# Two bursts of 38 and 40 down products in place of three (22, 32, 24) in the FP4 feed-forward stage

## The chip, the cores and the metric

The kernel runs on one core of a Trainium2 chip. That core has a tensor engine (PE in the profile, its weight loads PEld), a vector engine (DVE), a scalar engine (ACT), a general engine (POOL), each with its own instruction queue, and DMA queues (SP issues most transfers). The metric is the device time of one execution in microseconds.

## The reference, cut to what matters

The model has two layers on x of 2 x 1024 rows of 512. The change lies in the first layer's feed-forward block, whose weights are stored as 4-bit codes with one scale per group of 128 inputs:

```python
w_gu   = dequant_fp4(gate_up_packed, gate_up_scales)   # [2*1408, 512]
w_down = dequant_fp4(down_packed, down_scales)         # [512, 1408]
gate, up = split(x @ w_gu.T)                           # 1408 columns each
h = silu(gate) * up
y = h @ w_down.T
x = layernorm(x + y / sqrt(mean(y*y) + 1e-6))
```

Before it stands a linear attention, after it a second layer (gated linear attention, then a feed-forward over the top 512 rows of each sequence). Neither is touched.

## The kernel before, in words

**Blocks and steps.** The 2048 rows are four blocks of 512 (`blk`, NB = 4). In each block the 1408 hidden columns are eleven steps of 128 (`f`, NI = 11). A step (`scaled_sums`, L727) makes one 128x512 tile of gate and one of up. Each is a sum over four groups `k` of 128 inputs, and each group has its own scale, so each group's product goes to a PSUM bank of its own: two matmuls (the row tile is split into a high and a low part) and then an eviction. A step is thus 8 banks and 16 matmuls in the order gate, up for k = 0, 1, 2, 3. The evictions of k = 0 are on ACT (L740), those of k = 1 to 3 on DVE (L746: scale and add to the tile), six a step. Where `by_three` holds, the last one of up goes instead by ACT (L743) into a spare tile and by POOL (L744) into the sum. It holds in block 0 for the odd steps and from step 8 on, in blocks 1 and 2 from step 8 on, and never in block 3.

**Banks and rooms.** In this stage the ring `mm` has six of the eight PSUM banks and `acc` two (L903). A bank can be written again when its eviction is done, so the PE can be at most six banks ahead. Gate and up tiles have two rooms in blocks 1 to 3, taken in turn (L914): step f writes where step f-2 wrote, and so waits for the product that read it.

**End of a step.** ACT takes the SiLU of gate (L935), POOL multiplies it with up into `h` (L936, written `hm` below, `hm(3)` for step 3).

**Down products.** The down product of a block is done by a seven-product scheme (`down`, L771) while the next block's steps run. It is a generator that gives one matmul at a time, 78 in all: P1 10, P2 12, P5 10, P4 12, P6 10, P7 10, P3 12, P8 2. Its operands are sums of blocks of h that POOL makes, five instructions a sum (L797): S before P1, and after P5 (the first of them overwrites what P5 reads) three more sums, 15 instructions. It also needs sums of the down weights (`T1`, `T2`, `T4` and a new B12, eight POOL instructions, `sums_of_wdn` L722), made in steps 0 to 3 of block 1. Each P has one `acc` bank, in turn, so P5 uses P1's and P4 uses P2's. ACT copies P1 to y (L803), DVE adds the others (L805 to L827). The y tile of all blocks is one place.

**What sets the order.** The program writes it out: `issue_after` puts each step's matmuls behind the one before on PE, and the work below behind the step's last matmul, eviction, SiLU and `hm`. Apart from such edges each engine's order follows the order of the program among what is ready, as a scheduler fixes it before the run. At f = 0 one call starts `down` (the sums S). Then come the bursts:

```python
if blk > 1 and f in old_steps:
    old_steps[f]()
if blk and f in (1, 4, 7):
    take(pieces, {1: 22, 4: 32, 7: 24}[f])
    mm = last_p[0]
```

In blocks 2 and 3 `old_steps` (L883) finishes the block two before: at f = 0 the squares of y on ACT (L860) and their power on POOL (L864, L865); at f = 1 scaled y on ACT (L869) and four adds to x on POOL (`to_x`, L874); at f = 4 the row statistics on DVE (L187, L188); at f = 7 the normalisation of four tiles on POOL (L839 on DVE, L840, L843). At f = 8 and 9 the next block's rows are turned and split (L196, L210, L211), or in block 3 turned for the next stage (L652). After block 3 its own down products follow in seven parts of another order (L1000), which the change leaves as it is.

## Time and profile before

| | us |
|---|---|
| median of 3 runs (lowest to highest) | 966.21 (965.07 to 968.18) |
| the profiled execution, its own time | 965.93 |
| its span in the profile | 963.8 |
| step 2 to 4 of block 2, gate and up products | 371.47 to 382.86 |
| its second burst, 32 matmuls asked for | 382.86 to 396.49 |
| steps 5 to 7 | 396.49 to 407.88 |
| its third burst, 24 matmuls asked for | 407.88 to 418.05 |
| steps 8 to 10, and 0 and 1 of block 3 | 418.05 to 438.39 |

Each float32 matmul of the down products shows as two matmul records in the trace (22 asked for are 44 records). The PE's records overlap, as matmuls are pipelined: how long one occupies the engine is read from the distance of the starts, not from its duration. In a line of the timeline stand the start, the time from the first start to the last end, the engine, the source line, what is written from what, the count, and in brackets how long the engine had been idle and what released it.

### The profile page before, as it was taken

How to read it: one execution, taken by the hardware profiler on the slowest of the kernel's cores; microseconds unless marked ns; L12 is line 12 of the kernel's file. 1: busy time of each engine (PE TensorE's matmuls, PEld its weight loads, DVE VectorE, ACT ScalarE, POOL GpSimd, SP SyncE). 2: the span in 40 equal slices, each digit the busy share in tenths (PEclk: the TensorE clock that was granted, in tenths of full speed). 3: DMA queues.
4: the chain of work that ended last, by engine and by line, in shares of the span. 5: the costliest groups of instructions: out<-in, count | busy, mean ns of one | idle time of the engine just before them, and what ended most of it. 6: DMA issues, size and time to landing. Idle time of an engine off the chain costs nothing. (4 is left out here: it accounts for less than half of the span.)

```text
span 963.8 us, 11530 instructions
## 1 busy us (share of the span) xinstructions
PE 948.5 (98%) x4261; PEld 753.1 (78%) x4261; DVE 706.4 (73%) x1343; ACT 290.8 (30%) x498; POOL 310.5 (32%) x278
## 2 busy tenths in 40 slices
PE   9999999999999999999999999999999999999996
PEld 6668876785788888888887866778758688888886
DVE  3569986887995676676669485584997795898635
ACT  2244333342552254245133323322122033220000
POOL 1110184003787445576557320101052021000022
PEclk9999999999999999999999999999999999999999
DMA  9622212200000000000011230000005302150011
GB/s 325 211 76 89 83 57 68 67 1 0 2 1 1 1 1 1 1 1 1 1 44 45 100 141 1 1 1 0 1 29 168 110 22 67 45 175 1 1 44 44
DMA packets 25978, 48.77 MB, mean 51 GB/s; under 512 B 4684, under 2 KB 6732, under 8 KB 25411
## 3 DMA queue, kind: packets, MB, share of 16 engines
q1 hardware_dynamic: 23283, 42.92, 13.2%
q0 software_dynamic: 1920, 4.22, 1.2%
q10 hardware_dynamic: 720, 0.92, 0.3%
q8 instruction: 33, 0.54, 0.2%
q14 instruction: 22, 0.18, 0.1%
HBM read 39.63 MB, written 10.52 MB: 52 GB/s over the span
## 5 line engine op out<-in xcount | busy, mean ns | idle before, releaser
L180 POOL TENSOR_TENSOR rs<-rs,table 128x4 f32<-128x4 f32 (+1 forms) x21 | 19.7, 937 | 296.8 <-DVE rs L179 296.5
L746 DVE SCALAR_TENSOR_TENSOR gate<-gatep,scale,gate 128x512 f32<-128x512 f32 x123 | 91.4, 743 | 6.3 <-PE gatep L735 5.9
L746 DVE SCALAR_TENSOR_TENSOR up<-upp,scale,up 128x512 f32<-128x512 f32 x112 | 83.1, 742 | 0.1
L735 PE MATMUL gatep<-x1Th,wgu 128*128 128x512 f32 x176 | 72.4, 411 | 0.6 <-DVE x1Tl L211 0.6
L735 PE MATMUL upp<-x1Th,wgu 128*128 128x512 f32 x176 | 70.4, 400 | 0.1
L735 PE MATMUL upp<-x1Tl,wgu 128*128 128x512 f32 x176 | 69.0, 392 | 0.0
L735 PE MATMUL gatep<-x1Tl,wgu 128*128 128x512 f32 x176 | 68.9, 392 | 0.0
L740 ACT ACTIVATE gate<-gatep,scale 128x512 f32<-128x512 f32 x41 | 28.3, 691 | 110.3 <-PE gatep L735 104.0
L936 POOL TENSOR_TENSOR h<-up,gate 128x512 f32<-128x512 f32 x30 | 39.2, 1308 | 68.3 <-ACT gate L935 63.0
L782 PE MATMUL P<-wdn,h 128*128 128x256 f32 x256 | 60.5, 379 | 0.0
L782 PEld LDWEIGHTS P<-wdn,h 128*128 128x128 f32 x256 | 48.4, 190 | 6.7
L1150 POOL TENSOR_TENSOR sum<-sum,sq 128x512 f32<-128x512 f32 x12 | 19.7, 1644 | 80.4 <-issue 66.3
L1180 PE MATMUL go<-big 128*128 128x256 f32 x192 | 43.7, 381 | 0.0
L366 PE MATMUL xk<-pair,x 128*128 128x512 f32 x96 | 42.7, 592 | 0.0
L187 DVE BATCH_NORM_STATS2 st<-x 128x6 f32<-128x512 f32 x64 | 42.0, 674 | 0.4
L735 PEld LDWEIGHTS upp<-x1Th,wgu 128*128 128x128 f32 x176 | 33.0, 188 | 11.6 <-DVE up L746 3.6
L1180 PEld LDWEIGHTS go<-big 128*128 128x128 f32 x192 | 35.9, 190 | 5.8 <-issue 1.2
L735 PEld LDWEIGHTS gatep<-x1Th,wgu 128*128 128x128 f32 x176 | 33.1, 188 | 9.2 <-DVE gate L746 2.1
L735 PEld LDWEIGHTS upp<-x1Tl,wgu 128*128 128x128 f32 x176 | 33.1, 188 | 6.4 <-issue 0.2
L735 PEld LDWEIGHTS gatep<-x1Tl,wgu 128*128 128x128 f32 x176 | 33.1, 188 | 6.0
L782 PE MATMUL P<-T,S 128*128 128x256 f32 x160 | 35.8, 379 | 0.0
L782 PEld LDWEIGHTS P<-T,S 128*128 128x128 f32 x160 | 30.3, 190 | 4.2
(489 smaller groups left out, 2266.4 us busy)
## 6 DMA issues: line engine op xcount, KB each, us to landing
pk<-in_gu SPq DMA_DIRECT2D x16, 352.0 KB, 3.7
x<-in_x SPq DMA_DIRECT2D x4, 1024.0 KB, 13.0
w<-in_w SPq DMA_DIRECT2D x1, 4096.0 KB, 14.6
xs<-picked SPq DMA_DIRECT2D x4, 1024.0 KB, 5.1
out<-x SPq DMA_DIRECT2D x4, 1024.0 KB, 4.3
w<-in_w SPq DMA_DIRECT2D x4, 1024.0 KB, 7.3
x0T<-in_xT SPq DMA_DIRECT2D x3, 1024.0 KB, 7.9
pk<-in_dn SPq DMA_DIRECT2D x11, 256.0 KB, 3.4
```

The lines of the kernel that those rows point to most:

```text
L180: power = nc.gpsimd.tensor_tensor(rs[:, :n], rs[:, :n], const("mhalf")[:, :n], ALU.pow).ins
L187: nc.vector.bn_stats(st, x)
L366: ins = nc.tensor.matmul(acc_of[b][c], x_t[blk][:, i, c * P : (c + 1) * P], pairs_of["k", blk][i // 2][:, i % 2], start=blk % 2 == 0 and i ...
L735: ins = nc.tensor.matmul(ps, wgu[:, k, at * P : (at + 1) * P], x[:, k], start=x is parts[0], stop=x is parts[1]).ins
L740: nc.scalar.activation(acc, ps, AF.Copy, scale=s)
L746: last = nc.vector.scalar_tensor_tensor(acc, ps, s, acc, ALU.mult, ALU.add).ins
L782: last_p[0] = nc.tensor.matmul(cut, x(j)[:, r], w[:, j], start=j == 0, stop=j == NP - 1 and tail is None).ins
L936: hm = nc.gpsimd.tensor_mul(h.chunk(f), up, gate).ins
L1150: nc.gpsimd.tensor_add(sum2, sum2, sq)
L1180: ins = nc.tensor.matmul(ps[:, 256 * m : 256 * m + 256], w[:, k, m], b[:, k, 256 * half : 256 * half + 256], start=first and m == 0 and k ...
```

## The change

The three bursts behind steps 1, 4 and 7 become two behind steps 2 and 6, of 38 and 40 matmuls. The 78 matmuls are the same and in the same order. The first burst is now P1, P2, P5 and the first half of P4; the second is the rest of P4, then P6, P7, P3 and P8. What `take` draws from the generator besides matmuls moves with them: the evictions, and POOL's 15 sums behind P5, which now come at step 2 and not at step 4. The `old_steps` stay at 0, 1, 4 and 7.

```diff
-                    if blk and f in (1, 4, 7):
-                        take(pieces, {1: 22, 4: 32, 7: 24}[f])
+                    if blk and f in (2, 6):
+                        take(pieces, {2: 38, 6: 40}[f])
                         mm = last_p[0]
```

## The prediction

> **What bounds the kernel now.** First the page's busy shares and its costliest groups:

> ```profile
> PE 948.5 (98%) x4261; PEld 753.1 (78%) x4261; DVE 706.4 (73%) x1343; ACT 290.8 (30%) x498; POOL 310.5 (32%) x278
> ...
> L746 DVE SCALAR_TENSOR_TENSOR gate<-gatep,scale,gate 128x512 f32<-128x512 f32 x123 | 91.4, 743 | 6.3 <-PE gatep L735 5.9
> L746 DVE SCALAR_TENSOR_TENSOR up<-upp,scale,up 128x512 f32<-128x512 f32 x112 | 83.1, 742 | 0.1
> ```

> PE is never free, so nothing can be won by filling it; and the evictions on DVE wait for PE almost nowhere. Whether PE is at its own pace must be read by stretch. The busy time by stretch, for steps 2 to 4 of block 2 and the burst after them (columns: stretch, its length, then busy time of PE, PEld, DVE, ACT, POOL):

> ```profile
> 371.47:382.86 11.39, 11.39 (x50) 9.02 (x49) 10.23 (x16) 5.43 (x9) 2.61 (x2) 1.00 0.00 1
> 382.86:396.49 13.63, 13.63 (x66) 12.00 (x64) 6.34 (x14) 0.63 (x1) 11.10 (x17) 1.00 0.00 1
> ```

> In steps DVE is nearly as full as PE; in the burst it works 6.3 of 13.6 us. The timeline inside the steps shows who leads (start, length):

> ```profile
> 380.57 0.75 DVE L746 SCALAR_TENSOR_TENSOR up<-upp,scale,up 128x512 f32<-128x512 f32 x1
> ...
> 381.37 0.19 PEld L735 LDWEIGHTS upp<-x1Th,wgu 128*128 128x128 f32 x1 [0.36 <-DVE up L746]
> 381.37 0.50 PE L735 MATMUL upp<-x1Th,wgu 128*128 128x512 f32 x1
> ```

> The weight load waits for an eviction that began 0.80 us earlier and ends at 381.32: PE has run six banks ahead and is out of banks.

> **Paces.** Undisturbed gate and up matmuls start 0.2267 us apart in the timeline, so a bank takes PE 0.453 and a step of eight 3.63. DVE's evictions start 0.66 apart: six are 3.96. **In a step PE gains 0.33 us on DVE, and a burst is where DVE catches up.** After a burst the first DVE eviction starts 1.85 after the run's start (371.47, 373.32), an eviction ends 0.75 after its start, and PE writes bank n as soon as bank n-6 is out (0.05 later in the lines above). Changing from a burst to steps costs 0.19 (first two starts 371.47 and 371.89, 0.42 for 0.23). A run of three steps takes 11.39 for 3 x 3.63 + 0.19 = 11.08: 0.3 lost. A down matmul is 0.43 (32 in 13.63).

> **Part by part.** Removed: one switch per block, 3 x 0.19 = -0.6, and the two three-step runs' losses, 6 x 0.3 = -1.8. Work on no engine is removed or added. What moves:

> *Run between the bursts, steps 3 to 6.* Four steps: DVE's eviction number j (from 0) ends at 2.6 + 0.66 j. The last one that PE still needs is that of bank 24 (j = 17), 13.8; bank 30 follows, and three banks later the run ends: 13.87 + 1.36 = 15.2, against 4 x 3.63 + 0.19 = 14.7. **Block 1: +0.5.** In blocks 2 and 3 the row statistics of step 4 come on top. Before, they lie under the burst:

> ```profile
> 384.52 0.75 DVE L746 SCALAR_TENSOR_TENSOR up<-upp,scale,up 128x512 f32<-128x512 f32 x1
> 385.17 1.28 DVE L187 BATCH_NORM_STATS2 st<-x 128x6 f32<-128x512 f32 x2
> ...
> 387.77 0.65 DVE L807 TENSOR_TENSOR y<-y,P 128x512 f32<-128x512 f32 x1
> ```

> From 385.17 to 387.77, and a last aggregate of 0.1: 2.7 us. Queued behind them on DVE are the evictions of steps 5 and 6, for which PE waits. Bank 24 is then out at 16.5 and the run ends at 17.9, 3.2 over 14.7. The order on DVE matters little: the work is the same 4 x 3.96 + 2.7 before the run can end. **Blocks 2 and 3: 2 x 3.2 = +6.4.**

> *Normalisation of step 7, blocks 2 and 3.* Before, it starts in the third burst, and POOL's next work comes only 2.3 us after it:

> ```profile
> 410.42 1.28 POOL L936 TENSOR_TENSOR h<-up,gate 128x512 f32<-128x512 f32 x1 [2.52 <-DVE rs L839]
> 411.66 1.02 POOL L840 TENSOR_TENSOR rs<-rs,table 128x4 f32<-128x4 f32 x1
> 412.79 8.26 POOL L843 TENSOR_SCALAR x<-x,mv,rs 128x512 f32<-128x512 f32 x4
> 423.36 1.30 POOL L744 TENSOR_TENSOR up<-up,b 128x512 f32<-128x512 f32 x1 [2.32 <-ACT b L743]
> 425.57 1.30 POOL L936 TENSOR_TENSOR h_even<-up,gate 128x512 f32<-128x512 f32 x1 [0.91 <-ACT gate L935]
> ```

> Now steps 8, 9 and 10 follow at once. Count from the second burst's end. hm(7) starts at 6.4 (the hm of a first step after a burst: 371.47 to 377.85) and ends at 7.65, the power at 8.7; the four tiles fill 8.8 to 17.05. Behind them stand in block 2 the sum of L744 (1.25) and hm(8) (1.3): hm(8) ends at 19.6. Step 10 writes into the room that hm(8) reads, so ACT's k = 0 eviction of gate waits until then and ends 0.7 later, 20.35. PE reaches step 10 at 3.82 + 4.49 + 4.59 = 12.9 (steps 8 and 9 with their transposes: 418.05, 422.73, 427.32, less the switch), and its seventh bank, which needs the first one's room, 6 x 0.453 later, at 15.6. It waits until 20.4: **+4.8**. In block 3 there is no sum of L744: 19.15 for 15.6, **+3.5**.

> *Run over the block's edge, steps 7 to 2.* It grows by one step at each end. DVE waits 0.23 for PE at 432.73, at step 0, so lag from before it is gone there; steps 0, 1 and 2 are then a three-step run, +0.3 in blocks 1 and 2. In block 3 it starts full after the stall, +0.7. In blocks 2 and 3 the squares of step 0 keep ACT until 1.7 after step 1's end, over the k = 0 evictions of step 2 (due 0.7 after it): nothing if the SiLU of step 1 lets them first, 0.4 if not; I take the half, 2 x 0.2. **+1.7 in all.**

> *POOL's 15 sums* come two steps earlier. In the trace they run from 386.66 to 396.96, 10.3 us. The first may start once P5's second half has read its operand: 22 + 6 matmuls into the burst, 12.1, so they end at 22.4, 6.0 after the burst's end of 38 x 0.4314 = 16.4. The next on POOL, hm(3), is ready 6.4 after it. Free; without that cover they would hold hm(3) and, from two steps on, PE. In block 1 the five weight sums of step 1 end at 297.76, P5 starts only at 285.96 + 3.83 + 9.5 = 299.3: free.

> *The y tile.* P1's copy must wait for `to_x`:

> ```profile
> 371.49 0.59 ACT L803 COPY y<-P 128x512 f32<-128x512 f32 x1 [3.62 <-POOL x L874]
> ...
> 372.10 0.69 DVE L805 TENSOR_TENSOR y<-y,P 128x512 f32<-128x512 f32 x1 [7.61 <-ACT y L803]
> ```

> These 7.6 us of DVE look like the thing to win. They lie under the burst (ended 371.47), and DVE's next eviction still waited 0.53 for PE: the gain is 0. What is new is that P5 reuses P1's bank in the same burst. It starts at 365.8 + 9.5 = 375.3, the copy ends some 372.1: free, with 3 us to spare.

> **Sum.** -0.6 - 1.8 + 0.5 + 6.4 + 4.8 + 3.5 + 1.7 = +14.5. On the profiled execution's own 965.93 (its span and 2.1 around it) that is 980.4; it stood 0.3 under the median shown, so I predict 980.5. The matmuls after block 3 follow the steps without a gap, so I let all of it reach the end. Uncertain are the two POOL stalls (0 to 10 together: the order on POOL) and the half I took for the squares.

> **Rivals.**

> *POOL's order slips.* The order is fixed before the run by what is ready then. For it: on ACT the k = 0 evictions of a step stand ahead of the SiLU before. Against: all four tiles are ready together when the power is done, and stand earlier in the program than hm(8). If hm(8) goes between them, +8.3 falls: 972.1. Chance 0.17.

> *PE cools.* [...] The trace's longest gap is shorter:

> ```profile
> 589.85 3.72 PE L1180 MATMUL go<-big,Wog 128*128 128x256 f32 x16 [2.34 <-DVE uT L1216]
> ```

> after which the granted clock of that stretch (575 to 600) is 1.00. [...] By the row nothing: 980.4. The stalls are longer than the row's[...]; I take the row. Chance 0.12.

> *Faster: the lag does not grow with the run.* Place: DVE in steps 3 to 6 and POOL at step 7. For it: the five-step run over the block's edge loses hardly more than a three-step one. If the statistics moved under the second burst, hm(8) went first, and PE's six banks took up the rest, only the two removed terms would be left: 963.5. It decides from the point where DVE has nothing but evictions in a run, and even then bank 24 is out at 13.8 for a bank 30 due at 13.3; with part of it the result is no change, 965.7. Against: that edge run has steps of five evictions, these have six. Chance 0.08, half of it faster, half same.

> **Numbers.** Forecast 0.63, with a span of its own of 976 to 984; range 969 to 987, which holds the first two rivals, the 0 to 10 of the POOL stalls, and 1 us for the small terms. A change under 0.3% (2.9 us) cannot be told from none. Slower 0.92, same 0.04, faster 0.04.

> **What will show it.** In blocks 2 and 3: statistics on DVE between steps 4 and 5 with PE waiting on DVE L746 behind them, and a run of steps 3 to 6 near 17.9 (block 1: 15.2); POOL's normalisation right before hm(8), ACT's k = 0 eviction of step 10 released by POOL, and PE idle 4.8 and 3.5 there; no wait at P5 or P6. Wrong I would be if hm(8) precedes the tiles, if PE stands at P5 for the y copy, or if the clock falls.

## The result, and the profile after

The changed kernel takes **988.61 us** (median of 5 runs, 987.61 to 989.41), the kernel before 966.21 (5 runs, 965.00 to 968.18). The ratio is 1.0231, with a 95% interval of 1.0219 to 1.0243: slower. The prediction was 980.5, its range ended at 987. So 14.5 us were foreseen, and by the spans of the two profiled executions (986.5 against 963.8) 22.7 came.

From the page of the kernel after, the lines that answer to the groups shown before, and the two rows of slices for PE's busy share and its granted clock:

```profile
PE 959.4 (97%) x4261; PEld 757.3 (77%) x4261; DVE 706.1 (72%) x1343; ACT 290.7 (29%) x498; POOL 308.9 (31%) x278
...
PE   9999999999999999989998999999999999999997
...
PEclk9999999999999999989998999999999999999999
...
L746 DVE SCALAR_TENSOR_TENSOR gate<-gatep,scale,gate 128x512 f32<-128x512 f32 x123 | 91.2, 741 | 25.0 <-PE gatep L735 14.0
L735 PE MATMUL gatep<-x1Th,wgu 128*128 128x512 f32 x176 | 74.3, 422 | 11.2 <-ACT gate L740 7.5
```

PE is still "97% busy", one point less than before. That number hides nearly everything: idle time is 27.1 us where it was 15.3, so of the 22.7 lost about half is idleness (11.2 ahead of the gate matmuls, 7.5 of it released by ACT's eviction at L740). The other half is PE busy for longer with the same 4261 instructions. Part of that is PE running at DVE's pace (from 483.73 to 485.71, in step 6 of block 3, its banks start 0.66 us apart, as DVE's evictions do, and not 0.453), and part shows in the clock row, which was 9 throughout before and now has dips.

The first foreseen place, the run of steps 3 to 6 in blocks 1, 2 and 3 (stretch, its length, busy time of PE, PEld, DVE, ACT, POOL, then the granted clock):

```profile
306.12:321.46 15.34, 15.34 (x67) 11.87 (x66) 13.50 (x21) 6.63 (x11) 11.72 (x14) 1.00 0.00 1
382.86:401.60 18.74, 17.17 (x66) 12.85 (x65) 16.90 (x30) 6.85 (x11) 10.44 (x13) 0.91 0.00 1
469.89:487.86 17.97, 16.39 (x66) 11.56 (x65) 16.12 (x29) 6.82 (x11) 10.46 (x13) 1.00 0.00 1
```

They were put at 15.2, 17.9 and 17.9. Block 2 is 0.8 longer than block 3 and has a granted clock of 0.91. Inside it, the statistics on DVE, and then what PE does:

```profile
391.95 0.74 DVE L746 SCALAR_TENSOR_TENSOR up<-upp,scale,up 128x512 f32<-128x512 f32 x1
392.61 1.27 DVE L187 BATCH_NORM_STATS2 st<-x 128x6 f32<-128x512 f32 x2
...
395.20 0.71 DVE L746 SCALAR_TENSOR_TENSOR gate<-gatep,scale,gate 128x512 f32<-128x512 f32 x1
```

```profile
394.01 0.39 PE L735 MATMUL upp<-x1Tl,wgu 128*128 128x512 f32 x1
395.97 0.50 PE L735 MATMUL gatep<-x1Th,wgu 128*128 128x512 f32 x1 [1.57 <-DVE gate L746]
...
397.12 0.63 PE L735 MATMUL upp<-x1Tl,wgu 128*128 128x512 f32 x1
397.54 0.63 PE L735 MATMUL gatep<-x1Th,wgu 128*128 128x512 f32 x1
```

DVE leaves the evictions from 392.61 to 395.20, PE runs through its six banks and stands 1.57 us. That is the wait that was foreseen. What follows was not: from 397 on the starts are 0.42 apart instead of 0.23.

The second place, step 7's normalisation on POOL in block 2:

```profile
427.50 8.26 POOL L843 TENSOR_SCALAR x<-x,mv,rs 128x512 f32<-128x512 f32 x4
435.73 1.26 POOL L744 TENSOR_TENSOR up<-up,b 128x512 f32<-128x512 f32 x1
437.07 1.26 POOL L936 TENSOR_TENSOR h_even<-up,gate 128x512 f32<-128x512 f32 x1
...
438.36 0.69 ACT L740 ACTIVATE gate<-gatep,scale 128x512 f32<-128x512 f32 x1 [5.57 <-POOL h_even L936]
```

```profile
434.40 0.39 PE L735 MATMUL upp<-x1Tl,wgu 128*128 128x512 f32 x1
439.10 0.79 PE L735 MATMUL gatep<-x1Th,wgu 128*128 128x512 f32 x1 [4.32 <-ACT gate L740]
...
440.55 0.63 PE L735 MATMUL upp<-x1Tl,wgu 128*128 128x512 f32 x1
440.98 0.63 PE L735 MATMUL gatep<-x1Th,wgu 128*128 128x512 f32 x1
...
520.45 0.39 PE L735 MATMUL upp<-x1Tl,wgu 128*128 128x512 f32 x1
524.00 0.79 PE L735 MATMUL gatep<-x1Th,wgu 128*128 128x512 f32 x1 [3.16 <-ACT gate L740]
```

POOL takes the four tiles, the sum and then hm(8), in the order foreseen; hm(8) ends at 438.3, ACT evicts, and PE goes on at 439.10, 4.5 after it could have (434.40 and 0.23). Here too it goes on at half pace (440.55 to 440.98, 0.43 between starts). The last two lines are block 3: 3.3 after it could have. The granted clock, in four stretches and those after them (same columns; 0.50 is what the text calls half clock, 1.00 full clock):

```profile
393.49:396.90 3.41, 1.84 (x7) 0.90 (x7) 3.41 (x10) 0.10 (x1) 0.76 (x1) 1.00 0.00 0
...
434.48:437.90 3.42, 0.31 (x2) 0.00 (x0) 0.00 (x0) 0.00 (x0) 3.34 (x3) 1.00 0.00 0
437.90:444.72 6.82, 5.62 (x13) 4.46 (x14) 4.16 (x7) 4.37 (x7) 4.67 (x5) 0.50 0.00 0
519.82:523.23 3.41, 1.02 (x5) 0.51 (x3) 0.00 (x0) 0.00 (x0) 3.41 (x3) 1.00 0.00 0
523.23:530.06 6.83, 5.57 (x14) 4.01 (x15) 5.36 (x7) 4.97 (x12) 3.38 (x4) 0.50 0.28 66
608.57:611.98 3.41, 1.14 (x5) 1.04 (x6) 2.22 (x3) 1.31 (x3) 0.00 (x0) 1.00 0.00 0
611.98:615.40 3.42, 3.42 (x9) 2.71 (x9) 0.00 (x0) 0.00 (x0) 0.00 (x0) 0.50 0.00 0
```

Each stretch of half clock here follows one in which PE was busy for 1.84 of 3.41 us or less, and each is 3.41 us long or twice that; with the one from 396.90 to 400.3 they make 20.5 us. The last lies in the next stage, behind a gap of 2.33 us that the kernel before has too, without the half clock.

### The profile page after: what moved, and what is told of

Same layout as the page of the kernel before. It is cut to its first block, busy times and chain, and to the rows that moved or that the text cites. A ratio compares the mean times of both kernels' runs of the same rounds, so it can differ in the third digit from the quotient of the medians.

```text
span 986.5 us, 11532 instructions
## 1 busy us (share of the span) xinstructions
PE 959.4 (97%) x4261; PEld 757.3 (77%) x4261; DVE 706.1 (72%) x1343; ACT 290.7 (29%) x498; POOL 308.9 (31%) x278
## 3 DMA queue, kind: packets, MB, share of 16 engines
q1 hardware_dynamic: 23283, 42.92, 12.9%
## 5 line engine op out<-in xcount | busy, mean ns | idle before, releaser
L746 DVE SCALAR_TENSOR_TENSOR gate<-gatep,scale,gate 128x512 f32<-128x512 f32 x123 | 91.2, 741 | 25.0 <-PE gatep L735 14.0
L735 PE MATMUL gatep<-x1Th,wgu 128*128 128x512 f32 x176 | 74.3, 422 | 11.2 <-ACT gate L740 7.5
L746 DVE SCALAR_TENSOR_TENSOR up<-upp,scale,up 128x512 f32<-128x512 f32 x112 | 82.9, 740 | 0.7 <-ACT up L740 0.4
L735 PE MATMUL upp<-x1Th,wgu 128*128 128x512 f32 x176 | 72.6, 413 | 0.6 <-ACT up L740 0.5
L735 PE MATMUL upp<-x1Tl,wgu 128*128 128x512 f32 x176 | 70.4, 400 | 0.0
L735 PE MATMUL gatep<-x1Tl,wgu 128*128 128x512 f32 x176 | 70.4, 400 | 0.0
L740 ACT ACTIVATE gate<-gatep,scale 128x512 f32<-128x512 f32 x41 | 28.3, 690 | 141.4 <-PE gatep L735 121.6
L936 POOL TENSOR_TENSOR h<-up,gate 128x512 f32<-128x512 f32 x30 | 39.3, 1311 | 93.5 <-ACT gate L935 93.2
L735 PEld LDWEIGHTS gatep<-x1Th,wgu 128*128 128x128 f32 x176 | 33.9, 193 | 22.9 <-ACT gate L740 8.3
L735 PEld LDWEIGHTS upp<-x1Th,wgu 128*128 128x128 f32 x176 | 33.8, 192 | 15.0 <-DVE up L746 5.2
L1180 PE MATMUL go<-big 128*128 128x256 f32 x192 | 43.7, 381 | 0.0
L187 DVE BATCH_NORM_STATS2 st<-x 128x6 f32<-128x512 f32 x64 | 42.0, 674 | 0.4
L1180 PEld LDWEIGHTS go<-big 128*128 128x128 f32 x192 | 35.9, 190 | 5.8 <-issue 1.2
L735 PEld LDWEIGHTS upp<-x1Tl,wgu 128*128 128x128 f32 x176 | 33.9, 193 | 6.5 <-issue 0.2
L735 PEld LDWEIGHTS gatep<-x1Tl,wgu 128*128 128x128 f32 x176 | 34.1, 194 | 5.8
L1180 PE MATMUL go<-big,Wog 128*128 128x256 f32 x128 | 31.5, 399 | 3.1 <-DVE uT L1216 3.1
## 6 DMA issues: line engine op xcount, KB each, us to landing
x<-in_x SPq DMA_DIRECT2D x4, 1024.0 KB, 13.3
```

The lines of the kernel that those rows point to most:

```text
L187: nc.vector.bn_stats(st, x)
L735: ins = nc.tensor.matmul(ps, wgu[:, k, at * P : (at + 1) * P], x[:, k], start=x is parts[0], stop=x is parts[1]).ins
L740: nc.scalar.activation(acc, ps, AF.Copy, scale=s)
L746: last = nc.vector.scalar_tensor_tensor(acc, ps, s, acc, ALU.mult, ALU.add).ins
L936: hm = nc.gpsimd.tensor_mul(h.chunk(f), up, gate).ins
L1180: ins = nc.tensor.matmul(ps[:, 256 * m : 256 * m + 256], w[:, k, m], b[:, k, 256 * half : 256 * half + 256], start=first and m == 0 and k ...
```

## The experiments

Three questions were open: is the loss the loss of cover (and not the number of bursts); what does the half clock cost; and what is the rest of the 8.1 us that were not foreseen. Unless it says otherwise, an edit is one to the changed kernel. The first four ran beside the same 25 runs of the kernel before (median 966.92), the last three beside 16 (966.91).

### The statistics back under a burst

```diff
-                    4: self.stats,
+                    2: self.stats,
```

> Two bursts, row statistics moved from step 4 to step 2, so under the first burst again. Theory (uncovered statistics cost 3.2 us in each of blocks 2 and 3): the runs of steps 3 to 6 fall from 18.8 and 18.0 to 15.3, the half-clock window at 397 goes; 988.6 - 6.4 - 0.8 = 981.4, 979 to 983. Rival (only POOL's stall at step 10 costs, as DVE catches up later anyway): 988.

Measured: 981.98 (981.26 to 982.36), 1.0151 [1.0135, 1.0166]. The run of steps 3 to 6 in block 2:

```profile
383.84:399.18 15.34, 15.34 (x66) 11.87 (x65) 13.49 (x21) 6.62 (x11) 10.46 (x13) 1.00 0.00 2
```

It is block 1's 15.34 again: PE idles nowhere. So the statistics cost what stands between the two, about 2.6 us a block, and with it went the half clock behind them (granted clock 1.00, where it was 0.91).

### The normalisation back under a burst

```diff
-                    7: lambda: self.norm(range(4)),
+                    6: lambda: self.norm(range(4)),
```

> Two bursts, normalisation moved from step 7 to step 6, so under the second burst again. Theory: the waits of 4.5 and 3.3 us in step 10 go, and with them the half clock after them (some 5 us): 988.6 - 8 - 5 = 975.6, 973 to 977.5. Rival (half clock costs nothing by itself): 980.5. Rival (the second burst is too short for it): 985 and over.

Measured: 974.28 (973.98 to 976.01), 1.0078 [1.0063, 1.0093], so 14.3 us less than the changed kernel. The run of steps 3 to 6 of block 2 keeps its statistics, and the run from step 10 to step 2 of block 3 has lost its stall:

```profile
383.05:401.03 17.98, 16.41 (x67) 11.55 (x66) 16.13 (x29) 6.82 (x11) 10.46 (x13) 1.00 0.00 1
431.13:446.22 15.09, 15.09 (x67) 11.82 (x66) 14.43 (x22) 11.31 (x23) 11.00 (x12) 1.00 0.00 1
```

The first row is the uncovered statistics without half clock: 17.98 where 17.9 was predicted. PE stood 1.57 us there too (17.98 less 16.41 busy), and no half clock came of it (granted clock 1.00). The two stalls of step 10 carry the larger part of the loss, as predicted.

### Both

```diff
-                    4: self.stats,
-                    7: lambda: self.norm(range(4)),
+                    2: self.stats,
+                    6: lambda: self.norm(range(4)),
```

> Two bursts, statistics at step 2 and normalisation at step 6: both under a burst again. Theory (the whole loss is cover lost, not the longer runs): 965.7 us, 964.5 to 967, no half clock in the FP4 stage. Rival (runs of four and seven steps exhaust the six banks by themselves): over 970.

Measured: 968.96 (21 runs, 966.29 to 969.74), 1.0013 [1.0006, 1.0021]. Two bursts with their cover kept lose only some 0.1%. That is 2 us above the range expected and 1 below the rival's: nearly the whole loss was lost cover, but the fewer bursts bring nothing, and the longer runs cost a little (their terms follow below). The bursts of one block, first in the kernel before, then in this one:

```profile
438.39:447.69 9.30, 9.30 (x45) 8.19 (x44) 2.33 (x4) 4.83 (x11) 8.88 (x9) 1.00 0.00 0
459.08:472.70 13.62, 13.62 (x65) 11.99 (x64) 6.35 (x14) 0.63 (x1) 11.08 (x17) 1.00 0.00 1
484.09:494.27 10.18, 10.18 (x50) 8.95 (x48) 4.24 (x8) 0.63 (x1) 7.57 (x6) 1.00 0.08 5
```

```profile
444.02:460.24 16.22, 16.22 (x78) 14.28 (x76) 7.29 (x15) 3.67 (x6) 11.52 (x13) 1.00 0.00 1
475.59:492.67 17.08, 17.08 (x81) 15.03 (x80) 6.20 (x11) 0.63 (x1) 10.53 (x6) 1.00 0.03 2
```

The same 78 products take 33.10 us in three bursts and 33.30 in two. At 0.4314 each they would be 33.65: each burst ends some 0.19 early, and that is what the first gate matmul after it loses. A switch costs nothing.

### PE kept busy through the stalls

```diff
+                    n = {(5, 3): 3, (10, 2): (9, 7)[blk - 2]}.get((f, k), 0) if blk > 1 else 0
+                    if n:
...
+                        for _ in range(n):
+                            ins = nc.tensor.matmul(
+                                fill[:, :256], wdn[:, NI - 1, :P], wdn[:, NI - 1, :256], start=True, stop=True
+                            ).ins
+                        return ins
```

The added matmuls write a bank of `acc` that is free then; nothing reads them. They stand where PE would wait: three ahead of step 6, nine (block 2) and seven (block 3) ahead of the seventh bank of step 10.

> The changed kernel with product matmuls that nobody reads put on PE just ahead of where it stands still in blocks 2 and 3: 3 ahead of step 6 (1.3 us in a gap of 1.6), 9 and 7 ahead of the seventh bank of step 10 (3.9 in 4.5, 3.0 in 3.2). The waits themselves stay. Theory 1 (the 8 us beyond the forecast are the half clock that follows a PE gone quiet): no half-clock window in the FP4 stage, 980.5 us, 979 to 982.5 (the last if the gap in the next stage still cools PE). Rival (the 8 us are the backlog of DVE and POOL behind the stalls, and the half clock falls on time that PE waits anyway): 988.6 as before, or up to 990 where the added matmuls are in the way.

Measured: 984.03 (983.67 to 986.11), 1.0182 [1.0166, 1.0197]; mean granted clock of the profiled execution 0.999, and no half clock before the last matmul. This lies between the two expectations, and in the range of neither. Step 10 of blocks 2 and 3 in PE's timeline:

```profile
433.86 4.05 PE L936 MATMUL fill<-wdn 128*128 128x256 f32 x18
438.32 0.50 PE L735 MATMUL gatep<-x1Th,wgu 128*128 128x512 f32 x1 [0.42 <-ACT gate L740]
...
519.52 3.18 PE L936 MATMUL fill<-wdn 128*128 128x256 f32 x14
522.86 0.50 PE L735 MATMUL gatep<-x1Th,wgu 128*128 128x512 f32 x1 [0.15 <-ACT gate L740]
523.20 0.40 PE L735 MATMUL gatep<-x1Tl,wgu 128*128 128x512 f32 x1
524.57 0.50 PE L735 MATMUL upp<-x1Th,wgu 128*128 128x512 f32 x1 [0.97 <-ACT up L740]
```

The wait for hm(8) is as long as before, only filled, and the matmuls behind it go at full pace (from 439.24 to 439.93 their starts are 0.23 apart, where they were 0.43). So the half clock costs **4.6 us** (988.61 - 984.03; the spans of the two profiled executions, 986.5 and 981.9, say the same), and 3.5 of what was not foreseen (984.03 - 980.5) are in the queues. The last line shows a piece of these: a second wait, for the k = 0 eviction of up. The 20.5 us at a granted clock of 0.50 would have cost half their length, 10.2 (an estimate from the two), had PE been the bound all through them.

### Half as many of them

```diff
-                    n = {(5, 3): 3, (10, 2): (9, 7)[blk - 2]}.get((f, k), 0) if blk > 1 else 0
+                    n = {(10, 2): (5, 4)[blk - 2]}.get((f, k), 0) if blk > 1 else 0
```

As above, unread, and none ahead of step 6.

> As the kernel with the unread matmuls, but only 5 and 4 of them ahead of the seventh bank of step 10 and none ahead of step 6, so that about 2.4 and 1.5 us of PE's silence are left. Reading of the traces so far (a fixed window of 3.41 us in which PE works under some 42% is followed by half clock): half clock appears exactly where such a window falls, wherever the gap begins. [...] Time 984 to 988.

Measured: 986.72, a single execution. The step 10 stall of block 2 is down to a gap of 2.14 us, with no half clock behind it (from 440.88 to 441.57 the starts are 0.23 apart). The mean granted clock is 0.995, and two stretches of half clock remain ahead of the last matmul:

```profile
394.40:397.81 3.41, 1.83 (x7) 0.62 (x6) 3.41 (x10) 0.57 (x1) 0.31 (x1) 1.00 0.00 0
397.81:401.23 3.42, 3.42 (x9) 2.70 (x9) 3.42 (x6) 1.42 (x3) 1.31 (x1) 0.50 0.01 2
605.99:609.40 3.41, 1.08 (x10) 0.79 (x8) 3.27 (x5) 1.84 (x5) 0.00 (x0) 1.00 0.00 0
609.40:612.82 3.42, 3.42 (x9) 2.68 (x10) 0.00 (x0) 0.52 (x1) 0.00 (x0) 0.50 0.00 0
```

The first follows a gap of only 1.58 us. A gap of 2.14 us was harmless and one of 1.58 was not, so length alone does not decide. By windows it came out as expected: in the two ahead of half clock PE worked an estimated share of 0.35 and 0.26, in the two over which the gap of 2.14 us lay some 0.6 each (how this is read stands in the last section).

### Three bursts, statistics without cover

The kernel before, with one step moved:

```diff
-                    4: self.stats,
+                    5: self.stats,
```

> The kernel before, three bursts, with the statistics moved from step 4 to step 5 and so out from under the burst. Theory (cover, not the number of bursts): the run of steps 5 to 7 in blocks 2 and 3 goes from 11.39 to 14.0 (bank 16's eviction out at 12.6, three banks after it), 5.2 us in all, ratio 1.0055, up to 1.008 where a window cools. Rival (only runs of four and more steps feel it): 1.000 to 1.002.

Measured: 972.69 (972.03 to 973.31), 1.0056 [1.0040, 1.0071]. Its run of steps 5 to 7 in block 2:

```profile
397.34:411.37 14.03, 12.54 (x51) 8.71 (x50) 13.47 (x25) 5.04 (x8) 3.09 (x3) 1.00 0.00 1
```

It was 11.39 (396.49 to 407.88 in the table of before). So 2.6 us a block, 5.3 for two, come with three bursts as with two: lost cover, whatever the number of bursts.

### Four bursts

The kernel before, with the statistics kept ahead of a burst:

```diff
-                    4: self.stats,
+                    3: self.stats,
...
-                    if blk and f in (1, 4, 7):
-                        take(pieces, {1: 22, 4: 32, 7: 24}[f])
+                    if blk and f in (1, 3, 5, 7):
+                        take(pieces, {1: 22, 3: 16, 5: 16, 7: 24}[f])
```

> The kernel before with four bursts (behind steps 1, 3, 5 and 7, of 22, 16, 16 and 24) and the statistics at step 3, so everything still lies under a burst. Theory (a run loses by DVE's lag only from the third step on, and a change from burst to steps costs nothing by itself, as the kernel with both parts moved back shows): runs of two steps at 7.45 us and not 11.39 for three, 0.3 saved in each of six, 1.9 in all; 0.998 of before, 0.997 to 0.999. Rival (each change costs 0.19 as the prediction had it): 0.9985 to 1.000. Rival (POOL's sums in the shorter second burst hold up a step): over 1.002.

Measured: 965.91 (12 runs, 964.22 to 966.96), 0.9987 [0.9978, 0.9996]. The gain is about 1 us and small, but the interval leaves out no change at all: this version is ahead of both kernels. Its two-step run:

```profile
371.46:378.97 7.51, 7.51 (x35) 6.18 (x34) 6.35 (x10) 3.64 (x6) 1.13 (x1) 1.00 0.00 0
```

Two steps at 3.63 and the 0.19 of the start would be 7.45: DVE's lag has little time to grow. The measured ratio lies in the range of the theory and in that of the first rival, so it does not tell them apart; the bursts do. In block 3 the 78 products take 32.90 us in four bursts (437.91 to 447.21, 454.71 to 461.43, 468.94 to 475.65 and 483.14 to 493.31), 33.10 in three and 33.30 in two: each further burst takes 0.2 off the products, what the change to steps costs behind it. From block 1's first step to the last down products the trace is 1.5 us shorter than that of the kernel before. The change went the wrong way along this line.

## Why the prediction was right, and where it was wrong

The terms of the sum, against what the traces show. All but the last are read where the clock was full, the second wait and the edge into block 3 in the run with PE kept busy:

| term | predicted | measured |
|---|---|---|
| three switches fewer | -0.6 | 0 (33.10 and 33.30 us of bursts) |
| six three-step runs gone | -1.8 | -1.9 (11.39 each, as read before) |
| steps 3 to 6, statistics included, over 14.7 a run | +6.9 | +7.2 (15.34, 17.98, 17.97, each less 14.7) |
| wait at step 10, block 2 | +4.8 | +4.5 |
| wait at step 10, block 3 | +3.5 | +3.3, and +1.1 for a second one (523.20 to 524.57, less 0.23) |
| the runs over the block's edge | +1.7 | +2.8 (0.3, 0.4 and 2.1) |
| half clock | 0 | +4.6 (2.9 in this stage, 1.7 in the next) |

**Right.** The direction, its cause and its main sizes. The statistics, POOL's normalisation ahead of hm(8) and the two waits for it came where they were put and within 0.3 us each. The 15 sums, the y tile and P5's bank cost nothing, as said: PE waits at neither P5 nor P6. "Faster" and "POOL's order slips" fell.

**The step that failed: "By the row nothing: 980.4."** This priced the clock at nothing, and gave "PE cools" 0.12. The row (the line of the trace before, shown there) was a single gap of 2.34 us that had stayed at full clock. It could not carry that: the same gap, 2.33 us, is followed by half clock in the changed kernel (611.98). The term measured 4.6; without it the changed kernel takes 984.0, within the range stated. That half clock would follow the stalls of step 10, as the rival had it, no trace of before had shown; it came at both, the clock stayed down for 6.8 us behind each, and together they cost 2.1. The other two places, behind gaps of 1.57 and 2.33 us, were not foreseen at all.

Set against the run with PE kept busy, the trace places the 4.6 us so: 0.8 behind the statistics of block 2; 0.4 around step 10 of block 2 (the delay there is 1.5 by step 1 of block 3, but DVE was setting the pace by then, and 1.1 comes back by step 3); 1.7, the rest, around the end of block 3; 1.7 in the next stage. So 6.8 us of half clock cost 0.4 where DVE set the pace, and 3.4 us cost 1.7 in the next stage. The last 1.7 is not the change's alone: the kernel before has the same gap, and going by their granted clocks about half of its runs may pay it too (last section). The change's own doing is the 2.9 in this stage, and of that the 0.8 did not come each time: with the normalisation back under a burst the same gap of 1.57 us cooled nothing (granted clock 1.00).

**Mis-sized terms, some 3.5 us.** Of these only the first is tested by a run (with both moves taken back); the others are read from the traces.

- *The switch.* "-0.6" is nothing. The 0.19 seen at the start of a run was read without the other end, where the burst stops 0.19 sooner than its matmuls' pace gives. Besides, steps 3 to 6 lose 0.6 a block where 0.5 was said. For the version with both moves taken back the terms that remain add up to +0.1 (-0.6, -1.8, 3 x 0.5, and 0.3 + 0.3 + 2 x 0.2 at the edges); in its trace the stretch from block 1's first step to the stage's last down products is 1.3 longer than before.
- *The block's edge after the stall.* "+0.7" and a share of the squares was 0.9 for block 3; 2.1 came. After the wait all banks are full, so for steps 10 to 1 PE goes at DVE's pace (with PE kept busy, its banks start 0.66 apart from 440.42 to 441.74), and an eviction of k = 0 on ACT waits its turn behind a SiLU that waits for DVE (in the same run, the SiLU at 441.72, idle 1.36 before it for DVE, and the eviction at 442.26).
- *A second wait in block 3's step 10.* Not in the sum at all. ACT's order behind the released gate eviction is a SiLU and a square, and only then the eviction of up:

```profile
523.26 0.69 ACT L740 ACTIVATE gate<-gatep,scale 128x512 f32<-128x512 f32 x1 [4.57 <-POOL h_odd L936]
523.85 0.62 ACT L935 ACTIVATE gate<-gate 128x512 f32<-128x512 f32 x1
524.37 0.62 ACT L860 ACTIVATE rw<-y 128x512 f32<-128x512 f32 x1
...
524.98 0.68 ACT L740 ACTIVATE up<-upp,scale 128x512 f32<-128x512 f32 x1
```

In block 2 the same eviction follows the gate's at once (438.95 behind 438.36). "What is queued behind the waiting instruction" was asked of POOL and of DVE, but not of ACT.

The table adds up to 21.6 of the 22.7. Some 0.8 of what is left lies in steps 7 to 9 (13.03 and 13.11 in blocks 1 and 2, where 12.9 was said) and between block 3's end and the next stage (0.4); the last 0.3 is not placed.

## What to carry to other kernels

Before work is moved, list what the burst (or any stretch with one engine slack) hides besides what it is there for: here DVE's statistics and POOL's normalisation, which stayed at their steps while the bursts moved away, and they alone carry nearly the whole loss. Where a change makes a saturated PE stand, price the clock as well as the wait, and by more than one gap: here one of 1.57 us was followed by half clock in one run and not in another. A cost read at one end of a stretch (a slow first matmul) counts only after the other end has been read.

## What the hardware showed that was not expected

What decides seems to be how much of a window PE worked, not the longest gap. The share is an estimate from the starts of the matmuls and their pace: from 393.49 to 396.90 some six gate and up matmuls at 0.23 make 1.4 of 3.41, or 0.41. Read so, the four full-clock windows ahead of half clock in the changed kernel have shares of 0.41 (from 393.49), 0.05 (434.48), 0.26 (519.82) and 0.33 (608.57), and the two with half the added matmuls 0.35 and 0.26. Windows that stayed at full clock although they hold part of a gap have 0.65 and 0.53 (from 478.84 and 482.25 in the changed kernel, around its gap of 1.58 us) and some 0.6 twice (from 435.36 and 438.77 with half the added matmuls). One of about 0.40 did too (from 585.97 in the kernel before, whose grid is read from the half clock behind its last matmul, which begins at 961.44), so the bound is not sharp, or the reading isn't. A window at half clock was followed by another where PE worked 0.59 and 0.47 of it (from 437.9 and 523.2 in the changed kernel), and by full clock where it worked nearly all of it (from 396.9, 441.3 and 612.0), which goes with each stall of step 10 there bringing two.

By this a gap of 1.6 us can cool the PE if it lies whole within a window among waits for evictions (0.41 in block 2 of the changed kernel), and one of 1.58 in its block 3 did not, where it lay across two (0.65 and 0.53). The same work can come out either way: the gap of the next stage (2.33 to 2.34 us where it was read) was followed by half clock in the profiled runs of five kernels (granted clock 0.50 or 0.51 behind it: after, each of the two moves taken back alone, half the added matmuls, four bursts), and not in those of four (1.00 behind it before and with both moves taken back; with all added matmuls a mean of 0.999; with three bursts without cover its 16 matmuls took 3.72 us, where they take 5.41 at half clock).

**This is probably what spreads the runs of one kernel.** From the first matmul behind that gap to the end of the kernel it is 373.95 us in two traces without that half clock (before, three bursts without cover) and 375.6 to 375.7 in four with it (after, statistics back under a burst, half the added matmuls, four bursts): it costs 1.7 us there. Of the 25 runs of the kernel before, the 12 with a mean granted clock of 0.998 or 0.999 average 966.3 us, the 13 with 0.996 or 0.997 average 968.2, about as far apart. But the kernel before was traced in one execution only, without that half clock, so that its slower runs are those with it is not shown.
